# A fourth score tile in a fused attention and Fourier block, in memory taken from the descriptor scratch

## The chip, the cores and the metric

The kernel runs on one core of one Trainium2 chip. The metric is the device time in microseconds. Three runs of the kernel before gave 3810.2, 3811.16 and 3815.46 us; the median is 3811.16 us. Everything is float32.

## The reference, cut to what matters

Two layers on an image batch x of shape (2, 48, 48, 768). Layer 0 is global attention with relative positions; layer 1 mixes in the frequency domain. The change touches layer 0 only.

```python
def _L0_conv_ref(x, qkv_w, qkv_b, proj_w, proj_b, rel_pos_h, rel_pos_w):
    ...                                   # q, k, v: 24 heads (2 images x 12), S = 2304, hd = 64
    attn = jnp.einsum('bqc,bkc->bqk', q * scale, k)
    rel_h = jnp.einsum('bhwc,hkc->bhwk', r_q, Rh)
    rel_w = jnp.einsum('bhwc,wkc->bhwk', r_q, Rw)
    attn = (attn.reshape(B * nh, h, w, h, w) + rel_h[:, :, :, :, None] + rel_w[:, :, :, None, :]).reshape(B * nh, S, S)
    attn = jax.nn.softmax(attn, axis=-1)
    out = (attn @ v).reshape(B, nh, h, w, hd)
    ...
    return out @ proj_w + proj_b

# x is (2, 48, 48, 768); _gn is a group normalisation with 32 groups
x = x + _L0_conv_ref(_gn(x), ...)         # attention
x = x + _L1_conv_ref(_gn(x), ...)         # rfft2, two small block matmuls with gelu, irfft2
```

So every query row gets 2304 scores: the product of query and key, plus one relative term for the key's row and one for its column. Then come the softmax and the product with the values.

## The kernel before, in words

The two images go one after the other (`block_kernel`). Each passes through the attention, the output projection with the first Fourier step (`project_out`), and the spectral stage (`Spectral`).

**Attention.** `norm_transpose` loads x in six tiles, turns it on TensorE and normalises it into xnT. Three of those six loads use one and a half tiles of the score pool. Then come 108 units in the order of `order`: six head pairs (pr) x six groups of rows (g) x three thirds (x). A unit holds 128 query rows of two heads. One loop iteration n (line 496 on) does this for its unit:

- `scores` (line 354): TensorE multiplies queries and keys in five pieces of up to 512 keys and two heads, each into a PSUM bank of its own (ps_s; seven banks serve all such products). VectorE adds the piece to what stands in the unit's score tile s, writes it there, and takes the running maximum (the custom instruction s<-ps_s,s). A reduction then gives the negative maximum nm.
- `numerators`: ScalarE takes the exponential in place, four instructions, which also give the sums.
- TensorE does work for later units meanwhile: keys and values of the next head pair (ps_proj, ps_v), at x = 2 the queries of the group after next (ps_proj), at x = 0 the relative terms of the next group (ps_r). In the last head pair there is no next pair to project.
- `weigh` (line 417): TensorE multiplies the turned numerators pT of the unit two before with the values, into the one output bank ps_o.
- `squares` and `exchange` (lines 397 to 415): VectorE transposes blocks of 32 x 32 of s in place, and twelve transfers and four ScalarE copies bring these from s to pT; half of a unit's in its own iteration, half in the next.
- `finish`: ScalarE copies the output bank out, as the last of its work in the iteration.
- `new_unit` (line 340): GpSimd fills the score tile of unit n + 1 with the sum of the two relative terms, which it reads from rhw. These are two instructions, one a head (line 344). VectorE's first addition to the tile must come after it.

**Score tiles.** s has 2 x 2304 numbers a partition and comes from the pool `at_s` with three tiles. A tile is written by GpSimd, VectorE and ScalarE, and last read by the transfers and copies of its second half. So the fill of unit n + 1 can start only when the second half of unit n - 2 is out.

**Relative terms.** For a group of rows `relative` copies the products to rel. SP writes them to DRAM with a skew (t<-rel) and reads them back into rhw (rhw<-t), which has two tiles.

**Order.** Instructions of TensorE, VectorE, ScalarE and SP that go through `InOrder` keep the order of the program. The fills (`nc.gpsimd`) and the weight loads (`load_w`, `nc.sync`) do not: a planner places them when the program is built. It also gives tiles their addresses, pool by pool like a stack, and adds the waits. All transfers are issued by SP, whose queue is in order. Where pools of a later stage lie over those of an earlier one, the later tile waits for the earlier one's readers. In the attention, `at_pt` (two tiles pT) and the small tiles of the normalisation are placed above `at_s`.

**Memory.** The builder object `bacc.Bacc` reserves part of each partition for descriptors that GpSimd writes when it issues a transfer. The kernel before leaves its size at the default.

Of the kernel before, what the change touches and what calls it, by code (L numbers as in the profile page):

```python
# [162 lines left out]
def attention(tc, k, x_b, a, oT, inv_d, late, span, ps_b, ps_o):  # L163
# [11 lines left out]
    nc = tc.nc  # L175
    with ExitStack() as ctx:
        pool = lambda name, bufs, **kw: ctx.enter_context(
            tc.tile_pool(name=name, bufs=bufs, **kw)
        )
# [5 lines left out]
        keep = pool("at_keep", 1)  # L185
        outp = pool("at_out", 2)
        smallp = pool("at_small", 4)
        sp = pool("at_s", 3)
        dp = pool("at_dram", 3, space=DRAM)

        def bank(name):
# [863 lines left out]
def block_kernel(tc, a, out):  # L1055
    nc = tc.nc
    B = a["x"].shape[0]
    with ExitStack() as ctx:
# [20 lines left out]
        for b in range(B):  # L1079
# [5 lines left out]
            def late(fill=0):  # L1085
# [4 lines left out]
                else:  # L1090
                    ready[0].step()

            attention(tc, k, a["x"][b], a, oT, inv_d, late, span, ps_b, ps_o)
            with ExitStack() as ctx2:
                pool = lambda name, bufs, **kw: ctx2.enter_context(
# [116 lines left out]
```

## Time and profile before

| what | us |
|---|---|
| median of three runs | 3811.16 |
| the profiled execution, in all | 3818.63 |
| its span in the profile | 3816.8 |
| TensorE matmul busy | 3660.0 (96%) |
| VectorE busy | 2845.0 (75%) |
| ScalarE busy | 2516.4 (66%) |
| GpSimd busy | 1993.1 (52%) |
| mean granted TensorE clock | 0.978 of full |

The span by stages, from the windows of the trace (PE is matmul busy time):

| stage | from, to | PE busy of | clock |
|---|---|---|---|
| image 1: start | 0 to 150 | 129.4 of 150 | |
| image 1: five pairs, with projections for the next pair | 150 to 1219 | 1069.0 of 1069 | 1.00 |
| image 1: last pair | 1219 to 1455 | 207.6 of 236 | 0.94 |
| image 1: output projection | 1455 to 1655 | 182.1 of 200 | 0.95 |
| image 1: spectral | 1655 to 1910 | 247.1 of 255 | 0.97 |
| image 2: start | 1910 to 2050 | 126.8 of 140 | |
| image 2: five pairs | 2050 to 3123 | 1073.0 of 1073 | 1.00 |
| image 2: last pair | 3123 to 3360 | 195.8 of 237 | 0.93 |
| image 2: output projection | 3360 to 3560 | 184.2 of 200 | 0.97 |
| image 2: spectral | 3560 to 3816 | 245.0 of 256 | 0.96 |

How to read what follows. PE is TensorE's matmul, PEld its weight load, DVE VectorE, ACT ScalarE, POOL GpSimd, SP the queue that issues transfers. In a timeline a row gives start, length, engine, line, operation, output and inputs, the count of instructions merged, and in brackets the idle time before it with what ended it. Most instructions go through a helper and carry its line, L68; they are told apart by tile. A wait is attributed to what came last by the profile, so a name in a bracket can be that of another wait that ended at about the same time. Matmul ends are modelled.

### The profile page before, as it was taken

What the parts mean: (1) busy time and instruction counts of PE and PEld (TensorE: products, weight loads), DVE (VectorE), ACT (ScalarE), POOL (GpSimd) and SP (SyncE); (2) the same over time, 40 slices, a digit from 0 to 9 for tenths busy, and PEclk for the clock granted to TensorE, in tenths of its full rate; (3) what the DMA queues carried; (4) which work ended last, traced back from release to release, by engine and by line L of the source; (5) the groups of instructions that cost most, each with busy time, mean ns of one, the idle gap of its engine ahead of it and who ended that gap; (6) DMA issues with size and microseconds to landing.
All of it is one profiled execution on the core that took longest, in us unless ns stands there. A gap on an engine that the chain in (4) does not pass through costs nothing.

```text
span 3816.8 us, 83418 instructions
## 1 busy us (share of the span) xinstructions
PE 3660.0 (96%) x31520; PEld 2596.1 (68%) x31520; DVE 2845.0 (75%) x6692; ACT 2516.4 (66%) x3690; POOL 1993.1 (52%) x598
## 2 busy tenths in 40 slices
PE   8999999999999887999989999999999999879999
PEld 6677776767777665566666777777677776645665
DVE  4788888888888883335557988889888898833445
ACT  3688888888888882133237888888888888821331
POOL 2466666666666664412125666666666666633121
PEclk9999999999999998999989999999999999989899
DMA  3677777777777887633526777777777778885334
GB/s 103 144 176 167 174 170 170 173 163 178 166 176 166 171 190 184 165 101 110 167 81 143 172 173 168 177 165 174 164 177 166 173 171 170 194 189 151 103 103 134
DMA packets 497821, 607.00 MB, mean 159 GB/s; under 512 B 180493, under 2 KB 312973, under 8 KB 497422
## 3 DMA queue, kind: packets, MB, share of 16 engines
q1 hardware_dynamic: 497422, 601.69, 67.4%
q8 instruction: 250, 4.10, 0.5%
q14 instruction: 149, 1.22, 0.1%
HBM read 131.61 MB, written 87.67 MB: 57 GB/s over the span
## 4 chain that ended last, share of the span: by engine, by line
PE 84%; DMA 5%; DVE 4%; POOL 3%; SPq 2%; issue 1%; ACT 1%; POOLq 0%; DVEq 0%; ACTq 0%
PE ps_o L68 20%; PE ps_s L68 19%; PE ps_proj L68 14%; PE ps_v L68 8%; PE acc L68 7%; PE ps L948 4%; DVE s L68 3%; POOL s L344 3%; DMA pT<-s 2%; PE ps_z L892 2%; PE ps L920 2%; PE ps L924 2%; PE ps_u L983 2%; SPq L68 2%; PE ps_y L721 2%; PE ps_r L68 1%
## 5 line engine op out<-in xcount | busy, mean ns | idle before, releaser
L344 POOL TENSOR_TENSOR s<-rhw 128x2304 f32<-128x2304 f32 x432 | 1744.8, 4060 | 1144.6 <-DMA pT<-s 601.1
L68 DVE CUSTOM_DVE_ANT_0 s<-ps_s,s 128x512 f32<-128x512 f32 (+1 forms) x2160 | 1223.6, 633 | 371.7 <-issue 243.3
L68 ACT ACTIVATE s<-s,nm 128x1152 f32<-128x1152 f32 x864 | 1074.7, 1245 | 452.5 <-DVE nm L68 414.8
L68 DVE STREAM_TRANSPOSE s<-s 128x1152 f32<-128x1152 f32 x864 | 1111.8, 1344 | 5.5 <-ACT s L68 5.5
L68 ACT COPY pT<-s 32x1152 f32<-32x1152 f32 x864 | 993.2, 1150 | 19.5 <-DVE s L68 2.1
L68 PE MATMUL ps_o<-pT,v 128*64 128x128 f32 x15552 | 919.7, 278 | 47.9 <-DMA pT<-s 21.8
L68 PEld LDWEIGHTS ps_o<-pT,v 128*64 128x64 f32 x15552 | 867.8, 140 | 112.2 <-issue 53.8
L68 PE MATMUL ps_s<-kT,qT 64*128 64x512 f32 (+1 forms) x4320 | 918.5, 558 | 13.4 <-DVE mx L68 9.8
L68 PEld LDWEIGHTS ps_s<-kT,qT 64*128 64x128 f32 x4320 | 431.4, 186 | 450.7 <-issue 333.9
L68 PE MATMUL ps_proj<-xnT,w 128*128 128x384 f32 (+1 forms) x2016 | 597.0, 450 | 2.3 <-ACT gn_rstd L151 2.3
L68 PEld LDWEIGHTS ps_proj<-xnT,w 128*128 128x128 f32 x2016 | 360.8, 191 | 209.0 <-DVE mx L68 41.0
L68 PE MATMUL acc<-proj 128*128 128x384 f32 x864 | 287.5, 492 | 40.5 <-POOL proj L68 40.5
L742 DVE TENSOR_TENSOR x<-acc,x 32x384 f32<-32x384 f32 (+2 forms) x216 | 119.2, 553 | 277.3 <-PE acc L68 192.6
L68 PEld LDWEIGHTS ps_v<-w,xnT 128*128 128x128 f32 x2592 | 295.9, 193 | 21.2 <-DVE mx L68 21.2
L68 PE MATMUL ps_v<-w,xnT 128*128 128x128 f32 x2592 | 308.1, 279 | 0.0
L965 POOL TENSOR_TENSOR spectrum<-spectrum 128x480 f32<-128x480 f32 x80 | 96.3, 1204 | 345.0 <-DVE spectrum L964 186.6
L68 PEld LDWEIGHTS acc<-proj 128*128 128x128 f32 x864 | 165.8, 193 | 156.6 <-POOL proj L68 41.3
L728 ACT COPY y<-ps_y 112x384 f32<-112x384 f32 x96 | 45.9, 478 | 265.8 <-PE ps_y L721 248.7
L68 DVE DVE_READ_ACCUMULATOR2_ANT mx<- 128x1 f32 x2160 | 178.9, 83 | 0.0
L68 POOL TENSOR_TENSOR proj<-proj 128x2304 f32<-128x2304 f32 x12 | 60.6, 5052 | 197.5 <-DMA proj<-inv_d 169.7
L68 ACT ACTIVATION_READ_ACCUMULATOR s<-s,nm 128x1 f32 x864 | 161.1, 186 | 0.0
L928 ACT ACTIVATE spectrum<-ps,b 96x400 f32<-96x400 f32 x96 | 56.6, 589 | 147.7 <-PE ps L924 147.7
(97 smaller groups left out, 2099.6 us busy)
## 6 DMA issues: line engine op xcount, KB each, us to landing
pT<-s SPq DMA_DIRECT2D x2592, 144.0 KB
t<-rel SPq DMA_DIRECT2D x144, 189.0 KB
rhw<-t SPq DMA_DIRECT2D x144, 144.0 KB
y<-y_d SPq DMA_DIRECT2D x40, 360.0 KB
u_d<-spectrum SPq DMA_DIRECT2D x40, 360.0 KB
u<-u_d SPq DMA_DIRECT2D x48, 300.0 KB
xt<-in_x SPq DMA_DIRECT2D x12, 1152.0 KB
w<-in_qkv_w SPq DMA_DIRECT2D x36, 384.0 KB
```

The lines of the kernel that those rows point to most:

```text
L68: return lambda *args, **kw: self.tc.keep_in_program_order(op(*args, **kw))
L344: nc.gpsimd.tensor_tensor(s[:, h, :].rearrange("p (y x) -> p y x", x=HW), rhw[:, x, h, :HW][:, :, None].to_broadcast([P, HW, HW]), rhw[:, ...
L721: nc.tensor.matmul(ps[:YP, : 2 * SC], lhsT=k.fw, rhs=part[:, t0 : t0 + 2, ch], start=True, stop=True,)
L728: nc.scalar.copy(y1[:, :, ch], ps[:YP, : 2 * SC].rearrange("p (t c) -> p t c", c=SC))
L742: nc.vector.tensor_tensor(dst, acc[p : p + n, :UQ], dst, ALU.add)
L892: nc.tensor.matmul(ps[:BS, w * 96 : (w + 1) * 96], lhsT=self.y2[s, j][:, w, i * BS : (i + 1) * BS], rhs=k.fh, start=True, stop=True,)
L920: nc.tensor.matmul(ps[:BS, :400], lhsT=w1[:, wa, i, :], rhs=zf[:, 0, fs], start=True, stop=False,)
L924: nc.tensor.matmul(ps[:BS, :400], lhsT=w1[:, wb, i, :], rhs=zf[:, 1, fs], start=False, stop=True,)
L928: nc.scalar.activation(self.o1[:, ri, fs], ps[:BS, :400], AF.Gelu, bias=self.b1[:, n, ri : ri + 1])
L948: nc.tensor.matmul(ps[64 * r : 64 * r + 64, w * BS : (w + 1) * BS], lhsT=self.o1[:, ri, f0 : f0 + 64], rhs=w2[:, (0, 2, 1, 0)[2 * r + ri], ...
L965: nc.gpsimd.tensor_tensor(val, val, clip, ALU.subtract)
L983: nc.tensor.matmul(ps[: 2 * HW, :480], lhsT=k.ih, rhs=d2[:, c0 : c0 + 480], start=True, stop=True)
```

## The change

The pool of score tiles gets a fourth tile, and the builder is told to keep 1024 bytes a partition for descriptors written by GpSimd instead of the default. No instruction is added or removed in the source. The fourth tile lets the fill of unit n + 1 wait for unit n - 3 instead of n - 2. The tiles placed above the score pool move up.

```diff
@@ attention @@
         outp = pool("at_out", 2)
         smallp = pool("at_small", 4)
-        sp = pool("at_s", 3)
+        sp = pool("at_s", 4)
         dp = pool("at_dram", 3, space=DRAM)
@@ kernel @@
-    nc = bacc.Bacc("TRN2", target_bir_lowering=False, num_devices=1)
+    nc = bacc.Bacc("TRN2", target_bir_lowering=False, num_devices=1, dynamic_dma_scratch_size=1024)
```

## The prediction

> **What bounds the kernel now.** I read the windows of the whole span first, then the waits, then the timelines of TensorE, VectorE and GpSimd side by side at the places where TensorE has a gap. Columns of the windows: length, busy time and instructions of PE, PEld, DVE, ACT and POOL, then granted clock, DMA share, GB/s.
>
> ```profile
> 1000.00:1050.00 50.00, 50.00 (x441) 33.52 (x439) 44.00 (x105) 42.62 (x61) 32.32 (x8) 1.00 0.75 164
> 1300.00:1350.00 50.00, 45.87 (x423) 32.41 (x420) 44.64 (x107) 40.98 (x58) 33.96 (x9) 0.97 0.72 159
> 1500.00:1550.00 50.00, 50.00 (x156) 29.16 (x155) 18.27 (x33) 5.74 (x12) 17.98 (x10) 1.00 0.82 203
> ```
>
> The first row stands for five of the six head pairs of both images: TensorE is full at full clock. The row at 1300 stands for the last pair, which has no keys and values of a next pair to project; there TensorE has holes. The stages after the attention (third row) use no score tile.
>
> ```profile
> POOL s L344 <- DMA pT<-s: 601.1, 117, 25.9
> DVE s L68 <- POOL s L344: 82.1, 47, 22.7
> PE ps_s L68 <- DVE mx L68: 9.8, 9, 1.5
> ```
>
> GpSimd's fill (L344, two instructions of 4.06 us per unit) waits 601 us for transfers that still read the tile of three units ago. That is the wait the fourth tile removes. What follows from it is far smaller: VectorE waits 82 us for fills, and TensorE only 9.8 us visibly for VectorE. The question is how much of the 82 us lies on TensorE's chain.
>
> **The middle: almost nothing.** From one maximum (nm) to the next, units take 12.21, 12.21 and 13.08 us. TensorE's own work fills this: scores 4.07, projection 4.07, weighting 4.08, and 0.87 for the relative terms once per three units. Eight stretches of 18 units (units 6 to 78 of each image) take 226.31, 226.22, 227.03, 226.38 and 226.66, 226.22, 226.66, 226.63 us. The shortest, 226.22, is met twice, so I take it as TensorE's floor. The excess over it adds up to 2.35 us; its largest part, 0.81, holds the one clear stall by a late fill (at 812.64, 0.93 us). Bounds: 0 if the excess is not the fill, 2.35 if all is. I take **2.3**.
>
> **Start of each image.** Here the lower piece of unit 3 comes late:
>
> ```profile
> 117.23 16.14 POOL L344 TENSOR_TENSOR s<-rhw 128x2304 f32<-128x2304 f32 x4 [24.90 <-DMA pT<-s]
> 121.14 3.70 PE L68 MATMUL ps_s<-kT,qT 64*128 64x512 f32 x16
> 125.34 0.69 DVE L68 CUSTOM_DVE_ANT_0 s<-ps_s,s 128x512 f32<-128x512 f32 x1 [2.24 <-POOL s L344]
> 126.09 1.31 PE L68 MATMUL ps_s<-kT,qT 64*128 64x256 f32 x4 [1.25 <-DVE mx L68]
> ```
>
> GpSimd fills units 0 to 2 until 92.3, then waits for unit 0's transfers until 117.23. The second head of unit 3 is ready at 125.3, VectorE has stood for 2.24 us, TensorE runs out of banks. TensorE's scores of this unit last from 121.14 to 127.33, 6.19 us instead of 4.07. With a fourth tile, unit 3 needs only rhw of the next group, whose read is issued at 97.8; it is filled long before 121. TensorE's next work (four projections of keys, 16.4 us) waits for nothing, so 2.12 us are gained. The second image shows the same 6.19 (2024.22 to 2030.41). Sum **4.2**. The weighting before it (TensorE idle 1.32 us until 117.06 for unit 0's transfers) stays.
>
> **The last pair.** Here a wait named "POOL" must be split. When TensorE starts a unit's scores, VectorE's first piece starts 1.26 us later even with the tile long filled. A stall ahead of a first piece at that distance is TensorE's, whatever name it carries. A stall ahead of the second piece (second head) is a true late fill.
>
> ```profile
> 1280.83 5.80 PE L68 MATMUL ps_o<-pT,v 128*64 128x128 f32 x72 [2.90 <-ACT res L68]
> 1286.56 4.14 PE L68 MATMUL ps_s<-kT,qT 64*128 64x512 f32 x20
> 1298.77 4.98 PE L68 MATMUL ps_s<-kT,qT 64*128 64x512 f32 x20
> ...
> 1287.82 0.69 DVE L68 CUSTOM_DVE_ANT_0 s<-ps_s,s 128x512 f32<-128x512 f32 x1 [1.90 <-POOL s L344]
> 1301.69 0.69 DVE L68 CUSTOM_DVE_ANT_0 s<-ps_s,s 128x512 f32<-128x512 f32 x1 [0.96 <-POOL s L344]
> ```
>
> 1286.56 + 1.26 = 1287.82: the 1.90 us are not the fill's. TensorE was late because its weighting (1280.83) waited for ScalarE to empty the one output bank, and ran slowly. At 1298.77 + 1.26 = 1300.03 the first piece starts on time, and the second stands 0.96 us for the fill: true. True late fills that start a group of three: 1.26 (at 1264.68), 0.96, 1.05 (1338.83) in the first image, 0.70 (3167.59) and 2.25 (3204.38) in the second; sum **6.2**. Not counted: 0.27, 0.22 and 0.61 us (1238.64, 3189.99, 3253.16), since the next scores wait for the output bank by a chain through ScalarE that starts at the maximum of the unit before. Nor 2.04 and 0.37 (1413.65, 3316.31), where the weighting that follows waits for pT (TensorE idle 2.70 us ahead of it at 1418.41). Counting these adds 3.5; that is the upper end.
>
> Why VectorE does not simply run free: its floor is 10.87 us a unit (observed in every third unit), the pair averages 12.3, and 34 periods times 1.4 would promise 49 us. The chain that stays is: maximum, +11.05 ScalarE (four exponentials, relative copies, four pT copies, output copy), +5.8 weighting, +4.07 scores, +4.07 queries, +4.15 weighting, +1.26 and +5.65 VectorE = 36.05 us per group, against 37.0 measured. No fill is in it: about one microsecond a group is free, as counted above. Next in line behind the fill are the pT transfers, which let the fill start at 1293.58 while TensorE could use them at 1294.69.
>
> **Clock.** In the gap-and-weighting at 1280.9 to 1283.5 the granted clock is 0.50, after a gap of 2.90 us. The Trainium skill ("TensorE: Matmul & The Clock Gate", part 1) has the clock halved after an idle window of about 3.4 us, on a free-running window. By that rule a 2.90 us gap need not cool the array; by the trace it mostly does: in the last pairs eleven weightings take 5.5 to 7.0 us instead of 4.15, 21.6 us in excess, while one after the same 2.90 us gap (3183.73) takes 4.15. With the rule alone the sum would fall by up to 21.6 more; with the row it does not, because these gaps wait for ScalarE's output copy and pT, which the change does not touch. I take 0, and about 3 us either way for luck of the window.
>
> **The memory.** A score tile is 2 x 2304 x 4 = 18,432 bytes a partition. The Trainium skill ("SBUF — State Buffer", section on the size) has 224 KiB with 16 KiB kept for descriptors written by GpSimd; the change keeps 1 KiB, which frees 15,360. The tiles of the attention add up to about 207,700 bytes now and 226,100 then, against 228,352: it fits. What would speak against it is a ring too small:
>
> ```profile
> q1 hardware_dynamic: 497422, 601.69, 67.4%
> q8 instruction: 250, 4.10, 0.5%
> q14 instruction: 149, 1.22, 0.1%
> ```
>
> All data go by the hardware queue and every issue is SP's; by the rule a smaller ring could cost where GpSimd writes descriptors, by the row there is none: 0. If this cover were wrong it would touch every transfer. The pT tiles and the normalisation's tiles move up by 18 KB; in the second image they then lie over the first image's last y tiles, read until 1820, some 90 us before the loads that start the attention matter, and over unused space: 0.
>
> No instruction or transfer is added. The fill's only new possible wait is rhw, and behind it on GpSimd stand only later fills.
>
> **Sum.** 2.3 + 4.2 + 6.2 = 12.7 us. Of the profiled execution (span 3816.8, 3818.63 in all) this leaves 3805.9; against the median of 3811.16, 3.4 tenths of a per cent, it gives **3798.4 us**. A change under 0.2%, 7.6 us, could hardly be told from none.
>
> **Rivals.** (1) The wait moves: pT transfers or the output bank end last wherever the fill did. For it: TensorE starts that weighting only 1.1 us after the landing, and DMA is at 0.72 to 0.94 in the last pairs. Against: in the start and in three groups the next TensorE work is ready. Then only the start, or nothing: 3807 to 3811. It includes that the fourth tile is not used ahead because rhw arrives late.
> (2) Warm clock: closing gaps keeps the array at full clock in the last pairs as at 3183.73: 12.7 + 21.6 less, 3777. Against: the 2.90 gaps remain.
> (3) Slower: SP's order. SP's queue is in order, and weight loads (L197) are placed by the planner, not pinned. At 107.64 such a load stands ahead of unit 0's transfers, ready at 100.9, and holds them 6.7 us until its tile is free. If the planner, seeing other tile times, puts more of the 36 loads ahead of transfers, each can cost up to 6.7 us. Four that reach TensorE (26.8 - 12.7 = 14 us) end at 3825; from the third on (20.1 - 12.7) it is about 0.2% slower. Against: program order already has them there, and nothing in the code moved.
>
> **How the numbers follow.** Forecast 0.62 (own range 3792 to 3804), rival 1 0.22, rival 2 0.06, rival 3 0.10. Below 3803.5: 0.57 of the forecast and rival 2, 0.63. Within 0.2%: 0.05 of the forecast and rival 1, 0.27. Slower: 0.10. The range reaches from 3785 (the upper count of late fills, 16.2, lucky clock, some warm weightings) to 3812 (all of rival 1); left out are most of rivals 2 and 3.
>
> **What would show it.** Right: the fill's wait for pT falls from 601 us to a small rest; the second-piece stalls at unit 3 and in the last pair are gone; unit 3's scores take TensorE 4.1 us; middle periods stay 12.21/12.21/13.08; last-pair groups take about 36, not 37; the 2.90 us gaps ahead of weightings stay. Wrong: the fills start no earlier (the tile is not used), groups stay at 37 (another wait took the place), or periods near 10.9 in a row (ScalarE's chain does not bind).

## The result and the profile after

The changed kernel takes 3803.65 us, the median of eight runs, against 3813.61 us for eight runs of the kernel before: a ratio of 0.9969 with a 95% interval of 0.9958 to 0.9980. That is 0.31% faster; the two medians alone lie 10.0 us apart, 0.26%. The forecast was 3798.4 against 3811.16, 0.33%.

The windows of the span after, at the same places as before, with the same columns:

```profile
1000.00:1050.00 50.00, 50.00 (x441) 33.58 (x439) 43.30 (x104) 42.61 (x62) 34.10 (x9) 1.00 0.75 165
1300.00:1350.00 50.00, 43.20 (x440) 32.19 (x438) 48.20 (x114) 44.99 (x62) 32.77 (x9) 0.98 0.80 174
```

The middle is as full as before. In the last pair TensorE is busy for less of the window (43.20 against 45.87 us), yet it gets more instructions through (440 against 423), and VectorE is busy for 48.20 of 50 us instead of 44.64. A share of busy time would have read this the wrong way round, since slow matmuls count as busy in full: in the trace before, the 72 matmuls at 1280.83 are busy for 5.80 us at a granted clock of 0.50 and for 4.15 us at full clock, and the 20 at 1298.77, with VectorE late behind them, for 4.98 us instead of 4.14.

The waits after, first the total, then the number and the longest:

```profile
POOL s L344 <- DMA pT<-s: 452.8, 57, 15.1
POOL s L344 <- DMA rhw<-t: 386.7, 21, 84.8
DVE s L68 <- POOL s L344: 54.6, 21, 23.0
```

And the groups of the page, with the idle time just before them at the end:

```profile
L344 POOL TENSOR_TENSOR s<-rhw 128x2304 f32<-128x2304 f32 x432 | 1740.8, 4060 | 1114.1 <-DMA pT<-s 452.8
...
L68 PE MATMUL ps_s<-kT,qT 64*128 64x512 f32 (+1 forms) x4320 | 908.8, 557 | 6.6 <-DVE mx L68 3.9
```

The fills still take 4060 ns each and GpSimd still idles 1114 us ahead of them (1144.6 before). What changed is when it idles and for what: less for pT (601.1 before), more for rhw (151.4 before). TensorE's wait for VectorE ahead of scores is 3.9 us instead of 9.8.

The start of the first image, on TensorE and GpSimd:

```profile
118.02 4.15 PE L68 MATMUL ps_o<-pT,v 128*64 128x128 f32 x72 [1.23 <-ACT s L68]
122.10 4.14 PE L68 MATMUL ps_s<-kT,qT 64*128 64x512 f32 x20
126.17 9.30 PE L68 MATMUL ps_proj<-xnT,w 128*128 128x384 f32 x28
...
67.62 24.13 POOL L344 TENSOR_TENSOR s<-rhw 128x2304 f32<-128x2304 f32 x6 [66.17 <-DMA rhw<-t]
103.89 8.07 POOL L344 TENSOR_TENSOR s<-rhw 128x2304 f32<-128x2304 f32 x2 [12.14 <-DMA rhw<-t]
118.17 8.07 POOL L344 TENSOR_TENSOR s<-rhw 128x2304 f32<-128x2304 f32 x2 [6.21 <-DMA pT<-s]
```

Unit 3 is filled from 103.89, as soon as rhw of its group has landed, and no longer from 117.23. Its scores are one unbroken piece of 20 matmuls, 122.10 to 126.17, which is 4.07 us instead of 6.19.

In the middle GpSimd now works ahead in bursts:

```profile
1002.65 8.08 POOL L344 TENSOR_TENSOR s<-rhw 128x2304 f32<-128x2304 f32 x2 [0.77 <-DMA pT<-s]
1023.42 24.14 POOL L344 TENSOR_TENSOR s<-rhw 128x2304 f32<-128x2304 f32 x6 [12.69 <-DMA pT<-s]
```

And a group of three units in the last pair:

```profile
1277.55 4.15 PE L68 MATMUL ps_o<-pT,v 128*64 128x128 f32 x72 [2.90 <-DMA pT<-s]
1281.63 4.14 PE L68 MATMUL ps_s<-kT,qT 64*128 64x512 f32 x20
1285.69 4.14 PE L68 MATMUL ps_proj<-xnT,w 128*128 128x384 f32 x12
1290.06 4.15 PE L68 MATMUL ps_o<-pT,v 128*64 128x128 f32 x72 [0.22 <-DMA pT<-s]
1294.14 4.14 PE L68 MATMUL ps_s<-kT,qT 64*128 64x512 f32 x20
...
1346.59 5.82 PE L68 MATMUL ps_o<-pT,v 128*64 128x128 f32 x72 [2.90 <-DMA t<-rel]
```

The gap of 2.90 us ahead of a weighting is still there. This time the weighting behind it ran at 4.15 us (and at 1346.59 at 5.82 us); the next scores at 1294.14 are no longer stretched to 4.98 us.

Where the span's 14.6 us went can be added up from the start times of the 216 reductions nm, one a unit. The columns sum both images: from the maximum of unit 2 to that of unit 4, from 6 to 90, and from 90 to 107. The last column is the excess over 4.15 us of slow weightings in the last pair.

| kernel | 2 to 4 | 6 to 90 | 90 to 107 | slow weightings |
|---|---|---|---|---|
| before | 72.46 | 2114.29 | 419.36 | 23.1 |
| changed | 68.31 | 2112.07 | 412.61 | 23.5 |
| difference | 4.15 | 2.22 | 6.75 | |
| forecast | 4.2 | 2.3 | 6.2 | |

These make 13.1 us. The other 1.5 are a net of pieces that no step of the forecast names: 2.3 us less behind the last unit of the second image and 0.8 less ahead of the first units, against 1.6 more between the first two units of image 1 (18.42 instead of 16.78 us; most of the other kernels with three tiles have 18.4 there too).

### The profile page after: what moved, and what is told of

Read it like the earlier page. It is cut to its first block, busy times and chain, and to the rows that moved or that the text cites. A ratio compares the mean times of both kernels' runs of the same rounds, so it can differ in the third digit from the quotient of the medians.

```text
span 3802.2 us, 83341 instructions
## 1 busy us (share of the span) xinstructions
PE 3648.8 (96%) x31520; PEld 2592.3 (68%) x31520; DVE 2844.6 (75%) x6692; ACT 2519.5 (66%) x3692; POOL 1989.0 (52%) x598
## 3 DMA queue, kind: packets, MB, share of 16 engines
q1 hardware_dynamic: 497422, 601.69, 67.6%
## 4 chain that ended last, share of the span: by engine, by line
PE 89%; DMA 4%; ACT 3%; DVE 2%; issue 1%; SPq 1%; POOL 1%; POOLq 0%; DVEq 0%; ACTq 0%
PE ps_o L68 23%; PE ps_s L68 21%; PE ps_proj L68 15%; PE ps_v L68 7%; PE acc L68 7%; PE ps L948 4%; PE ps_z L892 2%; PE ps L920 2%; PE ps_u L983 2%; PE ps L924 2%; PE ps_y L721 2%; PE ps_r L68 1%; ACT pT L68 1%; PE ps_x L1001 1%; DMA pT<-s 1%; DVE s L68 1%
## 5 line engine op out<-in xcount | busy, mean ns | idle before, releaser
L344 POOL TENSOR_TENSOR s<-rhw 128x2304 f32<-128x2304 f32 x432 | 1740.8, 4060 | 1114.1 <-DMA pT<-s 452.8
L68 PE MATMUL ps_s<-kT,qT 64*128 64x512 f32 (+1 forms) x4320 | 908.8, 557 | 6.6 <-DVE mx L68 3.9
```

What stands on the lines that cost most here:

```text
L68: return lambda *args, **kw: self.tc.keep_in_program_order(op(*args, **kw))
L344: nc.gpsimd.tensor_tensor(s[:, h, :].rearrange("p (y x) -> p y x", x=HW), rhw[:, x, h, :HW][:, :, None].to_broadcast([P, HW, HW]), rhw[:, ...
```

## The experiments

The runs use the same two readings: time against the kernel before, and the columns above. The kernel before lay between 3814.75 and 3815.08 us in the three sets that follow.

**The reserve alone, and the fourth tile for some units alone.** Four kernels ran together. The first keeps three tiles and only shrinks the reserve:

```diff
-         sp = pool("at_s", 4)
+         sp = pool("at_s", 3)
```

> Three score tiles, and only the 1024 bytes for descriptors written by GpSimd. Theory (the late fills are the whole gain; nothing uses those descriptors): same as before within 0.2%, unit 3's scores again 6.19 us on TensorE in both images, GpSimd's wait for pT about 600 us. Rival (the smaller reserve moves addresses or transfers and is itself the gain): about 10 us below before.

Measured: 3814.68 us, ratio 1.0002 (0.9995 to 1.0009). In the trace unit 3 stands as before:

```profile
120.58 3.70 PE L68 MATMUL ps_s<-kT,qT 64*128 64x512 f32 x16
125.53 1.31 PE L68 MATMUL ps_s<-kT,qT 64*128 64x256 f32 x4 [1.25 <-DVE mx L68]
126.77 4.04 PE L68 MATMUL ps_proj<-xnT,w 128*128 128x384 f32 x7
```

126.77 - 120.58 = 6.19. The smaller reserve alone costs nothing and brings nothing that this interval could show.

The second gives the extra tile to unit 3 alone (the changed kernel's smaller reserve is kept; the pool has three tiles tagged s and one tagged s4):

```diff
-            s = sp.tile([P, 2, S], F32, tag="s", name="s")
+            n = (pr * (HW // 8) + g) * 3 + x
+            tag, bufs = ("s4", 1) if n == 3 else ("s", 3)
+            s = sp.tile([P, 2, S], F32, tag=tag, name="s", bufs=bufs)
```

> A fourth tile that only unit 3 of each image uses; all other units share three. Theory: unit 3's scores take TensorE 4.1 us instead of 6.19 in both images, so 4.2 us less; middle and last pair as before (excess of the middle about 2.3 us, late second heads in the last pair again). About 3809 where before is 3813.6. Rival (later units give the 2.1 us back, since weight loads or pT end last): maxima of units 4 to 6 no earlier than before, 0 us.

Measured: 3809.29 us, ratio 0.9985 (0.9978 to 0.9992), 5.5 us less. From unit 2 to 4 it takes 69.00 us, 3.5 less than before, and the units after it keep the lead. Not as expected, the middle and the last pairs of its trace are shorter too, by 2.0 and 3.7 us, though they still have three tiles. Unit 3's scores take 4.07 us:

```profile
120.61 4.14 PE L68 MATMUL ps_s<-kT,qT 64*128 64x512 f32 x20
124.68 10.59 PE L68 MATMUL ps_proj<-xnT,w 128*128 128x384 f32 x32
```

The third gives it to every fourth unit of the last pair:

```diff
-            tag, bufs = ("s4", 1) if n == 3 else ("s", 3)
+            tag, bufs = ("s4", 1) if n >= 90 and n % 4 == 2 else ("s", 3)
```

> A fourth tile that only units 90, 94, 98, 102 and 106 of each image use, so that the units of the last head pair wait for the tile of four units ago. Theory: 6.2 us less, plus or minus 3 for the clock; the stalls of VectorE ahead of a second head are gone in the last pair, unit 3 again 6.19 us. Rival (the wait moves to pT or the output bank): groups of three stay at 37 us, 0 to 2 us less.

Measured: 3806.04 us, ratio 0.9978 (0.9971 to 0.9986), 8.7 us less. Units 90 to 107 take 408.90 us instead of 419.36, and in the last pairs of both images in its trace no unit waits for a fill ahead of a second head. The 8.7 are 2.5 more than 6.2, within the margin given for the clock.

The fourth is the changed kernel again:

> The changed kernel again, beside its parts on the same chip. Theory: 10 to 13 us below before, and about the sum of the two parts above (10.4) plus 2.3 of the middle. Rival (one part makes the other useless): less than the larger of the two.

Measured: 3800.49 us, ratio 0.9964 (0.9951 to 0.9976), 14.3 us less, a little over what was expected. The two parts give 5.5 + 8.7 = 14.2. So they add, with little left for the middle: the runs with only one part also lost some of the middle's excess, with 2112.31 and 2112.95 us from unit 6 to 90, where the kernel before and the one with the smaller reserve have 2114.29 and 2114.07. All kernels with four tiles and the fill as it was lie at 2112.07.

The stalls ahead of a second head tell why. In the traces with three tiles such stalls for a fill add up to 2.65 us in the middle (before), 2.31 (smaller reserve), 0.22 (unit 3 alone) and 0.98 (last pair alone). The excess over TensorE's floor in units 6 to 78 is 2.34, 2.12, 0.38 and 0.99 us. The kernels with four tiles have no such stall there and 0.13 us of excess. Two of these stalls, of the kernel before and of the one with the tile for the last pair alone:

```profile
812.64 0.69 DVE L68 CUSTOM_DVE_ANT_0 s<-ps_s,s 128x512 f32<-128x512 f32 x1 [0.93 <-POOL s L344]
2478.14 0.69 DVE L68 CUSTOM_DVE_ANT_0 s<-ps_s,s 128x512 f32<-128x512 f32 x1 [0.98 <-POOL s L346]
```

So the middle's excess is the late fill's, as forecast; how often the fill is late with three tiles differs between these kernels.

**How near the fill was to being late everywhere.** The fill gets a third instruction that writes half of the second head again with the same numbers, 2.1 us in the trace:

```diff
+            nc.gpsimd.tensor_tensor(
+                s[:, 1, : S // 2].rearrange("p (y x) -> p y x", x=HW),
+                rhw[:, x, 1, : HW // 2][:, :, None].to_broadcast([P, HW // 2, HW]),
+                rhw[:, x, 1, HW:][:, None, :].to_broadcast([P, HW // 2, HW]),
+                ALU.add,
+            )
             return {"pr": pr, "g": g, "x": x, "qT": qT, "s": s}
```

> Three tiles as before; the fill gets a third instruction that writes the first half of the second head once more with the same numbers, 2.03 us more per unit. Theory (fill, scores, exchange and tile release form a ring of three units that was just inside TensorE's 12.5 us a unit): the ring needs about 13.1 us, so 0.3 to 0.8 us on each of some 200 units, 60 to 150 us slower. Rival (the fill has much room and the late ones are chance): under 15 us slower.

Measured: 3892.14 us, ratio 1.0203 (1.0189 to 1.0217), 77 us slower. The middle takes 2147.75 us (33.5 more), the last pairs 441.53 (22.2 more). The list of its waits shows many late fills, and TensorE short of banks:

```profile
DVE s L68 <- POOL s L350: 193.9, 138, 8.6
...
PE ps_s L68 <- DVE mx L68: 49.9, 37, 7.6
```

VectorE waits for the fill ahead of a second head in 86 of the 216 units, where the kernel before has 20; in the middle most of them are the first unit of a group. So with three tiles the fill was near the edge of the chain, in the middle once a group rather than in every unit. The ring's 13.1 us a unit were too many: the middle now takes 12.8 us a unit (1070.58 and 1077.17 us over 84), against 12.57 for TensorE's floor. About 23 of the 77 us come from the two image starts, and some of these are not the ring's: the order of the first fills, found in the next run, is in this kernel too.

> Four tiles, and the same 2.03 us more per fill. Theory: the ring of four units needs under 9 us a unit, and GpSimd's own 10.15 us is below VectorE's floor of 10.87; so within 4 us of the changed kernel. Rival (the fourth tile only hides a small lateness): over 20 us slower than the changed kernel.

Measured: 3817.57 us, ratio 1.0004 (0.9995 to 1.0013). That is some 17 us above the 3800.49 of the changed kernel in the set before, and not within 4. The steady state did as the theory said: the middle takes 2111.92 us, the lowest of all kernels, and the last pairs 413.85, as in the changed kernel (412.61 and 411.69). GpSimd there works through several units without a gap, ahead of need:

```profile
1001.50 8.07 POOL L344 TENSOR_TENSOR s<-rhw 128x2304 f32<-128x2304 f32 x2
1009.65 2.12 POOL L350 TENSOR_TENSOR s<-rhw 128x1152 f32<-128x1152 f32 x1
1011.73 8.08 POOL L344 TENSOR_TENSOR s<-rhw 128x2304 f32<-128x2304 f32 x2
```

The loss sits at the first unit of each image:

```profile
67.70 12.07 POOL L344 TENSOR_TENSOR s<-rhw 128x2304 f32<-128x2304 f32 x3 [66.25 <-DMA rhw<-t]
79.73 2.12 POOL L350 TENSOR_TENSOR s<-rhw 128x1152 f32<-128x1152 f32 x1
```

Three instructions of line 344 stand ahead of the first of line 350: the planner put the first head of unit 1 before the end of unit 0, and unit 0's maximum came 6 us late (86.97 against 80.81). The second image has the same 12.07 us ahead of its first L350 (at 1975.83). Pinning the fills to program order tests that:

```diff
-                nc.gpsimd.tensor_tensor(
+                gps.tensor_tensor(        # gps = InOrder(tc, nc.gpsimd), all three instructions
```

> Four tiles with the 2.03 us longer fill, and the fills pinned to the order of the program. In the run without the pin the third instruction of unit 0's fill stood behind unit 1's first (12.07 us of fill ahead of it), and unit 0's maximum came at 86.97 instead of 80.8. Theory (that order was the whole miss; the steady state has room for the longer fill): unit 0's maximum near 83, each start 2 us above the changed kernel, so 4 us above it in all and 8 us below before. Rival (the longer fill costs elsewhere too): still 12 us or more above the changed kernel.

Measured: 3806.00 us, ratio 0.9979 (0.9972 to 0.9986), 11.6 us below the unpinned one. Unit 0's maximum comes at 82.06. The changed kernel gave 3796.42 in the same set and 3800.49 in the one above, so the longer fill costs 5.5 to 9.6 us where 4 was expected. Most of the miss was the order; a rest of 2 to 6 us is not explained.

**The chain that stays.** If ScalarE's output copy is what the 2.90 us gaps wait for, it can be issued ahead of the four pT copies:

```diff
             evict(by_act)
+            if older is not None:
+                copy_out(older)         # act.copy of the output bank, taken out of finish()
             if last is not None:
                 squares(last, 1)
                 exchange(last, 1)
```

> Four tiles, and ScalarE copies the output bank out ahead of its four pT copies instead of behind them. Theory (the chain that stays in the last pair goes through this copy): the 2.90 us gaps of TensorE ahead of a weighting shrink to 1 us or less, some of these weightings run warm, groups go from about 35.5 to 33 to 34.5 us, 10 to 30 us below the changed kernel. Rival (pT lands last anyway): gaps stay above 2 us, under 5 us less.

Measured: 3791.22 us, ratio 0.9942 (0.9929 to 0.9954), 9.3 us below the changed kernel's 3800.49. Units 90 to 107 take 400.32 us, 12 less than in the changed kernel's two traces so far.

```profile
1274.52 4.15 PE L68 MATMUL ps_o<-pT,v 128*64 128x128 f32 x72 [1.07 <-DMA pT<-s]
1278.60 5.42 PE L68 MATMUL ps_s<-kT,qT 64*128 64x512 f32 x20
...
1308.23 4.15 PE L68 MATMUL ps_o<-pT,v 128*64 128x128 f32 x72 [1.02 <-DMA pT<-s]
```

In the first five groups of both images these gaps are 0.9 to 1.3 us, and every weighting behind one takes 4.15 us. What ends last ahead of them now is mostly pT. Ten gaps that shrink by 1.6 to 2.0 us would make about 18 us, and 12 were gained: among other things the scores behind such a weighting now take up to 5.47 us (5.42 at 1278.60) instead of 4.14.

> Three tiles, and the output copy ahead of the pT copies. Theory: the faster chain now meets the late fills, so only a part of the gain above is left, 3 to 12 us below before. Rival (the fills matter only through the chain that is now shortened): as much gained as with four tiles.

Measured: 3816.76 us, ratio 1.0002 (0.9993 to 1.0010): no gain, where 3 to 12 us were expected. Units 90 to 107 take 418.86 us, as before. The gaps shrink here too (0.98 and 1.07 us), but VectorE then meets the fill:

```profile
1303.07 0.69 DVE L68 CUSTOM_DVE_ANT_0 s<-ps_s,s 128x512 f32<-128x512 f32 x1 [2.25 <-POOL s L344]
```

Such stalls ahead of a second head add up to 15.8 us in its last pairs, against 11.0 in the kernel before. With three tiles the fill takes back all that the early copy gives.

To see how much of the early copy's gain was the clock's luck, the changed kernel and that version ran once more together:

> The changed kernel once more, to set beside the version with the early output copy. Theory: 10 to 14 us below before.

> Four tiles and the early output copy once more. Theory: 20 to 26 us below before and about 10 below the changed kernel, all of it in the last head pairs, groups of three at 34 us and the weightings at x = 1 at 4.15 us. Rival (the first result was the clock's luck): within 4 us of the changed kernel.

Measured: 3796.42 us, ratio 0.9951 (0.9939 to 0.9964), and 3794.58 us, ratio 0.9948 (0.9935 to 0.9962). The changed kernel lies 18.5 us below before, more than the 10 to 14 expected. The two are 1.8 us apart and not 10, as the rival said. In the traces units 90 to 107 take 406.72 and 402.01 us, with slow weightings of 16.2 and 7.3 us in excess. The changed kernel's three sets had medians of 3803.65, 3800.49 and 3796.42; the early copy's two had 3791.22 and 3794.58.

The traces tell what the early copy gains in the last pairs. Take the excess of the slow weightings off units 90 to 107, as a rough measure: 389.1, 389.0 and 390.5 us are left in the three traces of the changed kernel, 390.6 and 394.7 in the two of the early copy. So its last pairs are the shortest because fewer weightings are slow (9.8 and 7.3 us in excess against 16.2 to 23.5), and not because the chain itself got shorter. How much of that lasts from run to run is not settled. It is the fastest version that was run.

## Why the prediction was right

**The start** (4.2 forecast, 4.15 in the trace). Each step held: the fill needed only rhw, started at 103.89 instead of 117.23, and the four projections behind it had nothing else to wait for. The run with unit 3 alone gave 5.5 us with an interval that holds 4.2. That 4.15 lies so near 4.2 is luck: from unit 2 to 4 the traces with the fill as it was lie between 72.5 and 74.3 us without the tile and between 67.6 and 69.0 with it.

**The middle** (2.3 forecast, 2.22 in the trace). TensorE's floor of 226.22 us per 18 units was right: kernels with four tiles stay within 0.2 us of it over the eight stretches, 144 units. That the excess is the fill's was right too, by the stalls ahead of a second head (2.65 us of stalls for 2.34 of excess before, none with four tiles). The forecast named one of these stalls, 0.93 us; there were four more, of 0.21 to 0.56. What it could not see is that the excess belongs to this build: two other kernels with three tiles in the middle had 0.4 and 1.0 us of it.

**The last pair** (6.2 forecast, 6.75 in the first trace, 8.7 in the run that changes it alone). The test that mattered was to split a wait named "POOL" by its distance from TensorE's start. Ahead of the piece at 1287.82 stood 1.90 us that were not the fill's. Had the 49 us of a free VectorE, or the 54 us of all waits for fills but those of unit 0, been taken at their names, the forecast would have been four times too large. The early copy confirms the other half: with the fills out of the way it was this copy that held the gaps at 2.90 us.

The sum came out partly by luck. The first image gave 6.16 us and the second 0.59, where 3.27 and 2.95 were counted, because slow weightings fell by 3.1 us in the one and rose by 3.5 in the other. With their excess taken off, the last pairs go from 396.3 to 389.1 us. That is 7.2 us less, 3.1 in the first image and 4.1 in the second. The mechanism stands; its size is less sure. By the same measure kernels with three tiles there lie at 397.8 us (smaller reserve alone) and 392.5 (the tile for unit 3 alone), those with four and the output copy as it was at 388.7 to 390.5. The list of stalls ahead of a second head also missed one:

```profile
3328.57 0.69 DVE L68 CUSTOM_DVE_ANT_0 s<-ps_s,s 128x512 f32<-128x512 f32 x1 [1.30 <-POOL s L344]
```

And it counted eleven slow weightings, 21.6 us in excess; the trace has twelve with 23.1, the twelfth at 3331.72 behind a gap of 1.09 us.

**The memory** (0 forecast; a ratio of 1.0002, 0.9995 to 1.0009, measured with the smaller reserve alone). That the tiles above the score pool lie higher is not in this run, since it keeps three tiles; the runs with a fourth tile have it, and none of their traces shows a loss to put down to it.

**The rivals.** That the wait moves did happen within small limits (0.22 us for pT at 1290.06), and did not take the gain. The rival of the warm clock did not come either: 23.1 us of slow weightings in excess before, 23.5 after. SP's order changed only at the border of the images, where one load of constants comes earlier; ScalarE loads its tables there two more times (3692 instructions instead of 3690). No reading here shows either in the time.

**What was wrong.** "The fill's wait for pT falls from 601 us to a small rest": it fell to 452.8. An engine that runs ahead has the same work in nearly the same span, so its idle time stays; it came in fewer and longer waits (57 for pT instead of 117) and went in part to rhw. The right mark was the stalls of VectorE ahead of a second head, and those are gone but for the first unit of each image.

And "about 3 us either way for luck of the window" was too narrow. The three profiled executions of the changed kernel have slow weightings of 23.5, 22.7 and 16.2 us in excess, and single executions lie between 3789.21 and 3811.13 us. The granted clock goes with it: of the 21 executions of the changed kernel, the eight with a mean clock of 0.981 or more took 3789.21 to 3799.32 us, the eight with 0.978 or less 3800.43 to 3811.13. No run held the clock still. So the three gains of the changed kernel, 10.0, 14.3 and 18.5 us, surround the forecast of 12.7, and none of them is nearer the truth than this spread allows.

## What to carry to other kernels

A buffer is worth what its wait costs on the chain that sets the end, and not what the waiting engine idles: 601 us of GpSimd's idle time held about 13 us, found only where TensorE was held up too. Take each wait by the distance to the engine that feeds it before believing its name. And a buffer that is on the edge can block other improvements: here the early output copy brought nothing with three tiles, and with four the shortest last pairs of all, by fewer slow weightings.

## What the runs showed that was not expected

After a gap of 2.90 us, the same weighting of the same program takes 4.15, 5.82 or 7.06 us, and which it is changes from place to place and from execution to execution:

```profile
1241.47 5.81 PE L68 MATMUL ps_o<-pT,v 128*64 128x128 f32 x72 [2.90 <-ACT res L68]
1312.15 4.15 PE L68 MATMUL ps_o<-pT,v 128*64 128x128 f32 x72 [2.90 <-ACT res L68]
1382.67 7.06 PE L68 MATMUL ps_o<-pT,v 128*64 128x128 f32 x72 [2.90 <-ACT res L68]
```

All three are of the changed kernel, with the same gap and the same wait. What differs is where the gap lies. The granted clock in these traces changes only at steps of 3.41 us, on a grid that lies differently to the start of the program in each trace (from 0.10 to 2.85 us past it). Five of these steps, around the first and the second of these gaps (length, busy time and instructions of PE, PEld, DVE, ACT and POOL, then granted clock, DMA share, GB/s):

```profile
1238.48:1241.89 3.41, 0.51 (x9) 0.42 (x10) 3.38 (x14) 3.23 (x5) 0.00 (x0) 1.00 0.76 217
1241.89:1245.30 3.41, 3.41 (x38) 3.41 (x34) 3.41 (x4) 3.41 (x7) 0.00 (x0) 0.50 1.09 193
...
1306.74:1310.15 3.41, 2.41 (x10) 1.35 (x10) 3.41 (x13) 3.35 (x5) 1.89 (x1) 1.00 0.79 178
1310.15:1313.57 3.42, 1.42 (x26) 1.42 (x28) 3.39 (x11) 3.26 (x6) 0.00 (x0) 1.00 0.90 243
1313.57:1316.98 3.41, 3.41 (x54) 2.98 (x52) 3.41 (x3) 3.41 (x6) 0.00 (x0) 1.00 1.13 185
```

The first gap lies inside one step: TensorE is busy for 0.51 of 3.41 us, and the next step runs at half clock. The second is split over two steps with 2.41 and 1.42 us busy, and no half clock follows. Counted over the thirteen traces, all 338 steps in which TensorE is busy for less than 40% are followed by a step at half clock; from 40 to 80% it is 210 of 594, and above that 62 of 13,526. One step at half clock makes a weighting about 5.8 us, two make it about 7.

So whether a gap of 2.90 us slows TensorE depends on its place on a grid that the program does not choose. Two traces happen to have the same place, the changed kernel's first (2.85 us) and the one with the tile for the last pair alone (2.84 us): in the second image five weightings behind gaps of 2.90 us start within 0.02 us of each other and take the same 5.82, 7.07, 5.56, 5.82 and 5.49 us in both. A gap of about 1 us leaves most of a step busy: behind the gaps of 0.9 to 1.3 us of the early copy's first five groups every weighting took 4.15 us. No run moved a gap on the grid on purpose.
